# A graph layer with gathered rows: one more engine stops loading rows, and the gathers run further ahead

## The chip, the cores and the metric

The kernel runs on one core of a Trainium2 chip. A core has five engines that work side by side and wait for each other through semaphores: TensorE (PE in the profile; PEld is its weight load), VectorE (DVE), ScalarE (ACT), GpSimd (POOL) and SyncE (SP, which here only issues DMAs). The metric is the device time of one execution in microseconds; the median of three is given.

## The reference: what is computed

There are 12,500 nodes with 128 features each (x), and 200,000 directed edges (src, dst), sorted by dst. Per layer:

```
h    = max(layernorm(x), 0)                       # 12500 x 128
agg  = segment_sum(h[src], dst)                   # sum of the rows of all incoming edges
agg  = agg / max(deg, 1)                          # mean; deg counts the incoming edges
h    = relu(agg @ Wg + h @ Ws + bg)               # 128 -> 128
h    = tanh(h @ W1 + b1)                          # 128 -> 512
h    = tanh(h @ W2 + b2)                          # 512 -> 512
out  = x + h @ W3 + b3                            # 512 -> 128
```

The costly part is h[src]: 200,000 rows of 512 bytes, fetched in an order that only the data knows.

## The kernel before

**Table.** The layer norm is computed for all nodes in pieces and written to a table in DRAM, htab. All fetches of h[src] read it, so no row can be fetched from it before its last piece is written.

**Chunks.** The edges are cut into 1,563 chunks (NCH) of 128. For each chunk, the 128 rows h[src] come to lie on the 128 partitions of a tile, and a one-hot matrix (built by DVE from dst, eight chunks, a group, at a time) says which node each row belongs to. One PE matmul (line 297, function `add`) then adds the rows to the sums of a window of nodes, in PSUM. Because the edges are sorted, chunk c's window lies near node 8c; a window that touches two blocks goes to an `edge` sum first, which `merge` adds to both later. In the trace each such fp32 matmul shows as two passes.

**How rows arrive.** There are four ways.

- 80 chunks (10 groups of eight, in steps of 40 chunks from chunk 256) are `raw`: POOL gathers rows of x itself, while the table isn't ready yet, and DVE and ACT normalize them afterwards (`centre`, `factors`, `raw_scaled`).
- Most chunks are gathered from the table by POOL, one indirect DMA of 128 rows for each (function `gather`, line 310). The tiles come from a pool of AHEAD buffers, and a gather is recorded when `behind`, the count of such chunks added, is less than AHEAD back.
- 23 chunks (`slow_s`) are loaded by SP, one plain DMA for each row (function `row_loads`): the row's address is read into a register (line 344) and the row is copied (line 306).
- 15 chunks (`slow_a`) are loaded in the same way by ACT (line 335).

The lists of slow chunks are laid out at the head of `windowed`. The calls of `next(loading, 0)` and `next(loading_a, 0)` in the main loop spread the row loads: SP's come 32 at a time, ACT's four at a time. Each kind has two buffers.

**Blocks and layers.** The nodes are cut into blocks of 512 (at the end smaller ones). When all chunks of a block are added, its layers (`part0` to `part4`) are woven into PE's order, two or so matmuls between chunk matmuls. `count` sums the one-hots into degrees and takes their reciprocal; `own` loads a block's own rows from the table on SP and `own_turned` transposes them on PE (line 300), since h @ Ws needs them with features on partitions. The own rows of the next block are loaded 52 chunks, and turned 10 chunks, before the end of a span of 64 chunks, with one buffer (`hb`).

**What sets the order.** PE's matmuls, ACT's operations and SP's DMAs (`pe`, `act`, `sp_dma`) are kept in the order in which the loop records them. POOL's queue holds the 80 raw gathers and then all the others. From chunk QUICK = 1376 on, the loop weaves by a small model of time, in which the k-th gather arrives at 7.5 + 1.251 k us. A store of a block's output is recorded LATE = 12 chunks after its result. A block's layers are recorded LEAD = 10 chunks after its last chunk, if that lies before QUICK.

Of the kernel before, what the change touches and what calls it, by code (L numbers as in the profile page):

```python
# [22 lines left out]
F32 = mybir.dt.float32  # L23
# [8 lines left out]
P = 128  # L32
EPS = 1e-5
CPR = 16
BLK = 512
PIECE = 14
GRP = 8
NRAW = 10
RAW0 = 256
STEP = 40  # L40
AHEAD = 32
SLOW0 = 120
EACH = 58
EACH_A = 76
TOGETHER = 4
LOADS = 32
LATE = 12
LEAD = 10
QUICK = 1376

WINDOWS = ((0, 144), (1496, 88), (1536, 56), (1552, 40))
# [9 lines left out]
def windowed(ctx, tc, x, src, dst, Wg, Ws, bg, W1, b1, W2, b2, W3, b3, out, flag):  # L61
    nc = tc.nc
    N, D = x.shape
# [18 lines left out]
    def raw(c):  # L82
        return RAW0 <= c < RAW1 and (c - RAW0) % STEP < GRP


    slow_s, slow_a = [], []
    ns, na = 0, EACH // 2
    for c in range(SLOW0, NCH - 12):
        if raw(c):
            continue  # L90
        if ns <= 0:
            slow_s.append(c)
            ns = EACH
        elif na <= 0 and c < QUICK:
            slow_a.append(c)
            na = EACH_A
        else:
            ns -= 1
            na -= 1
    slow = slow_s + slow_a  # L100


    def first(w, span=per):
# [8 lines left out]
    blocks, n = [], 0  # L112
# [7 lines left out]
    dram = ctx.enter_context(tc.tile_pool(name="dram", bufs=1, space=bass.MemoryType.DRAM))  # L120
    const = ctx.enter_context(tc.tile_pool(name="const", bufs=1))
    raws = ctx.enter_context(tc.tile_pool(name="raws", bufs=1))
    rows_one = ctx.enter_context(tc.tile_pool(name="rows_one", bufs=2))
    rows_in = ctx.enter_context(tc.tile_pool(name="rows_in", bufs=AHEAD))
    ps_c = ctx.enter_context(tc.tile_pool(name="ps_c", bufs=1, space=PSUM))
    ps_a = ctx.enter_context(tc.tile_pool(name="ps_a", bufs=2, space=PSUM))
# [7 lines left out]
    for t, a in ((rsrc, src), (rdst, dst)):  # L134
        a = a[RAW0 * P : RAW1 * P].rearrange("(u e) -> u e", u=NRAW)[:, : GRP * P]
# [13 lines left out]
    raw_rows = []  # L149
# [29 lines left out]
    def spread(f, k):  # L179
        return f[:, :, None].to_broadcast([P, k, D])  # L180

    def centre(pool, xt, k, stats):
        nc.vector.tensor_reduce(stats[:, 0], xt, AX.X, ALU.add)
        nc.vector.scalar_tensor_tensor(xt, spread(stats[:, 0], k), -1.0 / D, xt, op0=ALU.mult, op1=ALU.add)
        sq = pool.tile([P, k, D], F32, name=f"sq{k}")
        nc.scalar.activation(sq, xt, AF.Square)
        nc.vector.tensor_reduce(stats[:, 1], sq, AX.X, ALU.add)

# [7 lines left out]
    with tc.tile_pool(name="setup", bufs=1) as sp, tc.tile_pool(name="ln", bufs=2) as ln:  # L196
# [32 lines left out]
        for i, (t0, k) in enumerate(pieces):  # L229
            xt = ln.tile([P, PIECE, D], F32, name="xt", bufs=3)  # L230
# [9 lines left out]
            stats = ps_a.tile([P, BLK], F32, name="agg")[:, : 2 * k].rearrange("p (s t) -> p s t", s=2)  # L240
            xt = xt[:, :k]
# [14 lines left out]
        for c0, w in WINDOWS[1:]:  # L256
            v = low[:, c0:]
# [31 lines left out]
    ed = ctx.enter_context(tc.tile_pool(name="ed", bufs=3))  # L289
    ml = ctx.enter_context(tc.tile_pool(name="ml", bufs=2))  # L290
# [14 lines left out]
    def sp_dma(*a):  # L305
        tc.keep_in_program_order(nc.sync.dma_start(*a))  # L306
# [10 lines left out]
    ROWB = 4 * D  # L317
    hbytes = htab.rearrange("n d -> (n d)").bitcast(U8)
# [3 lines left out]
    place = const.tile([len(slow), P], I32, name="place")  # L322
    nc.vector.tensor_scalar(place, at_i, float(ROWB), None, op0=ALU.mult)

    class act:
# [5 lines left out]
        def copy(*a):  # L331
            tc.keep_in_program_order(nc.scalar.copy(*a))  # L332

        def dma(*a):
            tc.keep_in_program_order(nc.scalar.dma_start(*a))  # L335

    def row_loads(chunks, engine, dma, name, together):
        for c in chunks:
            i = slow.index(c)
            r = rows_one.tile([P, D], F32, name=name)  # L340
            rows_t[c] = r
            rb = r.bitcast(U8)
            for p0 in range(0, P, LOADS):
                loads, vs = nc.values_load_multi_w_load_instructions(  # L344
                    place[i : i + 1, p0 : p0 + LOADS], engines=[engine], min_val=0, max_val=(N - 1) * ROWB,
                    skip_runtime_bounds_check_because="src holds rows of x, as the indirect DMAs take it to",
                )
                for ld in loads:
                    tc.keep_in_program_order(ld)
                for p, v in enumerate(vs, p0):  # L350
                    dma(rb[p : p + 1, :], hbytes[bass.ds(v, ROWB)].rearrange("(o b) -> o b", o=1))
                    if (p + 1) % together == 0:
                        yield

    def raw_stats(i):
        return stats_raw[:, :, i * GRP : (i + 1) * GRP]

    def raw_scaled(i):
        h = raw_rows[i]
        scale(h, h, GRP, raw_stats(i))  # L360
        for j in range(GRP):
            rows_t[RAW0 + i * STEP + j] = h[:, j]
# [32 lines left out]
    reach = [[] for _ in blocks]  # L395
# [84 lines left out]
    def own(s):  # L480

        n0 = s * BLK
        n = min(BLK, N - n0)
        k = -(-n // P)
        hb = ml.tile([P, BLK // P, D], F32, name="hb", bufs=1)
        sp_dma(hb[:, :k], htab[n0 : n0 + k * P, :].rearrange("(t p) d -> p t d", p=P))
        owns[s] = hb

    def own_turned(s):

        k = -(-min(BLK, N - s * BLK) // P)
        hb = owns.pop(s)
        pt = ps_t.tile([P, BLK // P, P], F32, name="pt")
        for t in range(k):
            pe.transpose(pt[:, t, :], hb[:, t, :], ident)
        hT = ml.tile([P, BLK], F32, name="hT")
        act.copy(hT[:, : k * P], pt[:, :k, :].rearrange("p t n -> p (t n)"))
        hTs[s] = hT
# [96 lines left out]
    def one_by_one(*parts):  # L595
        for part in parts:
            yield from part()

    def layers(b, before):
# [3 lines left out]
        last = [] if before is None else [part(part3, before), part(part4, before)]  # L603
        if reach[b][-1] + LEAD < QUICK:
            return one_by_one(
# [4 lines left out]
        )  # L610

    order = [c for c in range(NCH) if not raw(c) and c not in slow]
    loading = row_loads(slow_s, mybir.EngineType.SP, sp_dma, "srows", LOADS)
    loading_a = row_loads(slow_a, mybir.EngineType.Activation, act.dma, "arows", TOGETHER)
    work, done, nxt, behind = [], 0, 0, 0
    ngrp = -(-NCH // GRP)
    span = BLK // per
    now = at = 0

    def store(upto):  # L620
        while stores and stores[0][0] <= upto:
            sp_dma(*stores.pop(0)[1:])
# [5 lines left out]
    def go_on(w):  # L628
        nonlocal now
        if w:  # L630
# [3 lines left out]
            if w[1] is None:  # L634
                work.remove(w)

    own(0)
    own_turned(0)
    onehot(0)
    onehot(1)  # L640
    counted = 0
    for c in range(NCH):
        g = c // GRP
        at = c
        store(c if c >= QUICK else c - LATE)
        if c % GRP == 0 and g + 2 < ngrp:
            onehot(g + 2)
            if raw((g + 2) * GRP):
                raw_scaled(((g + 2) * GRP - RAW0) // STEP)
            if 2 <= g < 2 + NRAW:  # L650
                centre(ed, raw_rows[g - 2], GRP, raw_stats(g - 2))
            if g == 2 + NRAW:
                factors(stats_raw)

        while c % GRP == GRP // 2 and counted < len(blocks) and reach[counted][-1] // GRP <= g + 1:
            count(counted)
            counted += 1
        while nxt < len(order) and nxt < behind + AHEAD:
            gather(order[nxt])
            nxt += 1  # L660
        if not raw(c) and c not in slow:
            behind += 1
            batch = behind * P // (EACH * LOADS)
            if behind > SLOW0 - 2 * EACH and batch > (behind - 1) * P // (EACH * LOADS):
                next(loading, 0)
            batch = behind * P // (EACH_A * TOGETHER)
            if behind > 48 and batch > (behind - 1) * P // (EACH_A * TOGETHER):
                next(loading_a, 0)
        if c >= QUICK:

            there = 7.5 + 1.251 * (NRAW * GRP + order.index(c)) if c not in slow else 0
            while soonest() and max(now, soonest()[2]) < there:
                go_on(soonest())
            now = max(now, there) + 0.27
        add(c)

        lead = LEAD if c < QUICK else 2
        if done < len(blocks) and (c - lead if across[done] else c) >= reach[done][-1]:
            if across[done]:
                merge(done)  # L680
            quick = reach[done][-1] + LEAD >= QUICK

            before = done - 1 if done and reach[done - 1][-1] + LEAD < QUICK else None
            work.append([layers(done, before), 0, 0, 0, quick and blocks[done][1] <= P])
            done += 1
        if (c // span + 1) * BLK < N:
            if c % span == span - 52:
                own(c // span + 1)
            if c % span == span - 10:
                own_turned(c // span + 1)  # L690
        if c < QUICK:
            if c % 2 == 0:
                go_on(work[0] if work else None)
        if c == QUICK:
            for b, (_, n) in enumerate(blocks):
                if n < BLK:
                    own_part(b)
# [379 lines left out]
```

## Time and profile before

| what | value |
|---|---|
| median of three executions | 1931.07 us (1930.7 to 1931.43) |
| profiled execution, device time | 1931.2 us |
| its span, first to last instruction | 1928.7 us |
| PE / DVE / ACT / POOL busy | 67% / 55% / 12% / 75% |
| gathers from the table on POOL | 1,445 |
| row loads on SP / on ACT | 2,944 / 1,920 |
| mean granted PE clock | 0.866 |
| DMA, mean rate | 72 GB/s |

How to read the profile: "idle before" of a group is the time for which its engine stood idle just before those instructions, with what was released last; a line number is that of the kernel before, and one line can be that of a helper which records many operations, so tiles tell more than lines. `rows` are gathered tiles, `srows` and `arows` those loaded by SP and ACT, `hb` own rows, `raw` the rows of x. For an indirect DMA, POOL's busy time is the time it takes to issue it; the data land later. The digits of a slice are tenths of busy time in one fortieth of the span.

### The profile page before, as it was taken

How to read it: one execution, taken by the hardware profiler on the slowest of the kernel's cores; microseconds unless marked ns; L12 is line 12 of the kernel's file. 1: busy time of each engine (PE TensorE's matmuls, PEld its weight loads, DVE VectorE, ACT ScalarE, POOL GpSimd, SP SyncE). 2: the span in 40 equal slices, each digit the busy share in tenths (PEclk: the TensorE clock that was granted, in tenths of full speed). 3: DMA queues.
4: the chain of work that ended last, by engine and by line, in shares of the span. 5: the costliest groups of instructions: out<-in, count | busy, mean ns of one | idle time of the engine just before them, and what ended most of it. 6: DMA issues, size and time to landing. Idle time of an engine off the chain costs nothing.

```text
span 1928.7 us, 24991 instructions
## 1 busy us (share of the span) xinstructions
PE 1299.0 (67%) x5212; PEld 819.1 (42%) x5212; DVE 1066.8 (55%) x651; ACT 228.1 (12%) x362; POOL 1442.0 (75%) x1533
## 2 busy tenths in 40 slices
PE   0056487775757678758775676566776746878787
PEld 0034354443535445534443344344443424554466
DVE  7964865555556856636544465354554536645430
ACT  1100111010101111111100110001101101101122
POOL 7777777777777777777777777777777777777774
PEclk9999688898878888888887898878988879879698
DMA  8822222222222222222222222222222222222221
GB/s 202 233 65 53 55 67 59 61 71 60 67 71 66 66 70 67 71 71 61 65 61 66 71 61 65 61 71 66 61 66 66 61 70 61 71 78 71 66 62 40
DMA packets 128692, 139.69 MB, mean 72 GB/s; under 512 B 35036, under 2 KB 103294, under 8 KB 128336
## 3 DMA queue, kind: packets, MB, share of 16 engines
q0 software_dynamic: 48800, 100.04, 20.5%
q1 hardware_dynamic: 72654, 33.65, 6.4%
q10 hardware_dynamic: 7076, 4.32, 0.9%
q14 instruction: 119, 0.97, 0.2%
q8 instruction: 43, 0.70, 0.2%
HBM read 125.07 MB, written 12.82 MB: 71 GB/s over the span
## 4 chain that ended last, share of the span: by engine, by line
DMA 31%; PE 28%; issue 17%; SPq 11%; DVE 5%; POOL 3%; ACTq 3%; ACT 1%; POOLq 0%; DVEq 0%
PE pm L297 16%; DMA rows<-htab,scol 16%; SPq L306 10%; PE agg L297 6%; DMA arows<-htab 5%; PE edge L297 4%; DMA srows<-htab 4%; POOL rows L310 3%; DMA hb<-htab 3%; ACTq L335 3%; DVE cnt L392 2%; DMA xt<-in_x_dram 2%; PE pt L300 1%; DVE oh L382 1%; SPq L344 1%
## 5 line engine op out<-in xcount | busy, mean ns | idle before, releaser
L310 POOL DMA_INDIRECT rows<-htab,scol x1445 | 1363.4, 944 | 440.8 <-issue 258.9
L297 PE MATMUL pm<-h,w 128*128 128x512 f32 (+4 forms) x1344 | 649.1, 580 | 26.3 <-ACT h L329 26.3
L297 PE MATMUL agg<-oh,rows 128*128 128x144 f32 (+3 forms) x2068 | 484.4, 342 | 219.9 <-DMA rows<-htab,scol 217.1
L297 PEld LDWEIGHTS agg<-oh,rows 128*128 128x128 f32 x2068 | 360.7, 215 | 530.1 <-DMA rows<-htab,scol 395.2
L382 DVE TENSOR_TENSOR oh<-shared,dloc 128x1152 f32<-128x1152 f32 (+2 forms) x186 | 243.4, 1314 | 605.8 <-PE edge L297 354.9
L392 DVE TENSOR_REDUCE cnt<-oh 128x200 bf16<-128x1600 f32 (+2 forms) x186 | 525.8, 2832 | 5.4
L297 PEld LDWEIGHTS pm<-h,w 128*128 128x128 f32 x1344 | 223.4, 206 | 42.2 <-ACT h L329 29.4
L297 PEld LDWEIGHTS edge<-oh,rows 128*128 128x128 f32 x822 | 150.3, 219 | 160.5 <-issue 85.8
L297 PE MATMUL edge<-oh,rows 128*128 128x144 f32 (+2 forms) x822 | 181.8, 333 | 39.7 <-DMA rows<-htab,scol 39.4
L300 PE MATMUL pt<-ident,hb 128*128 128x128 f32 x98 | 24.5, 398 | 242.7 <-DMA hb<-htab 242.7
L329 ACT ACTIVATE h<-pm,b2c 128x512 f32<-128x512 f32 (+4 forms) x112 | 70.8, 632 | 447.6 <-PE pm L297 229.3
L300 PEld LDWEIGHTS pt<-ident,hb 128*128 128x128 f32 x98 | 16.8, 204 | 246.3 <-issue 246.3
L153 POOL DMA_INDIRECT raw<-in_x_dram,rsrc x80 | 77.7, 971 | 25.4 <-issue 23.8
L329 ACT ACTIVATE h<-pm,b1c 128x512 f32<-128x512 f32 (+4 forms) x112 | 69.9, 632 | 203.2 <-PE pm L297 107.3
L419 DVE RECIPROCAL rd<-rd 128x512 f32<-128x512 f32 (+4 forms) x28 | 81.8, 2920 | 0.0
L332 ACT COPY hT<-pt 128x512 f32<-128x512 f32 (+1 forms) x25 | 14.4, 577 | 410.2 <-PE pt L300 383.9
L589 DVE TENSOR_TENSOR o<-pt,xb 128x512 f32<-128x512 f32 x23 | 15.8, 688 | 75.9 <-PE pt L300 75.9
L417 DVE TENSOR_SCALAR rd<-pm 128x512 f32<-128x512 f32 (+4 forms) x28 | 17.2, 616 | 63.1 <-PE pm L297 63.1
L212 PE MATMUL pm<-ident,idx_f 98*128 98x98 f32 x32 | 6.2, 376 | 62.0 <-DVE idx_f L208 55.7
L297 PE MATMUL pm<-mT,wg 128*128 128x512 f32 (+4 forms) x56 | 32.6, 669 | 22.7 <-DVE mT L533 22.5
L329 ACT ACTIVATE h<-pm,bgc 128x512 f32<-128x512 f32 (+4 forms) x28 | 17.7, 632 | 240.0 <-PE pm L297 144.1
L297 PE MATMUL pm<-hT,ws 128*128 128x512 f32 (+4 forms) x56 | 34.8, 711 | 0.0
(72 smaller groups left out, 496.9 us busy)
## 6 DMA issues: line engine op xcount, KB each, us to landing
srows<-htab SPq DMA_DIRECT2D x2944, 0.5 KB
arows<-htab ACTq DMA_DIRECT2D x1920, 0.5 KB
rows<-htab,scol POOLq DMA_INDIRECT x1445
hb<-htab SPq DMA_DIRECT2D x24, 256.0 KB
xb<-in_x_dram SPq DMA_DIRECT2D x23, 256.0 KB
out_dram<-o SPq DMA_DIRECT2D x23, 256.0 KB
htab<-h SPq DMA_DIRECT2D x6, 896.0 KB
xt<-in_x_dram SPq DMA_DIRECT2D x5, 896.0 KB
```

The lines of the kernel that those rows point to most:

```text
L153: nc.gpsimd.indirect_dma_start(out=t[:, j, :], out_offset=None, in_=x, in_offset=bass.IndirectOffsetOnAxis(ap=rsrc[:, g, j : j + 1], axis=0),)
L297: tc.keep_in_program_order(nc.tensor.matmul(*a, **k))
L300: tc.keep_in_program_order(nc.tensor.transpose(*a, **k))
L306: tc.keep_in_program_order(nc.sync.dma_start(*a))
L310: nc.gpsimd.indirect_dma_start(out=r, out_offset=None, in_=htab, in_offset=bass.IndirectOffsetOnAxis(ap=scol[:, c : c + 1], axis=0),)
L329: tc.keep_in_program_order(nc.scalar.activation(*a, **k))
L335: tc.keep_in_program_order(nc.scalar.dma_start(*a))
L344: loads, vs = nc.values_load_multi_w_load_instructions(place[i : i + 1, p0 : p0 + LOADS], engines=[engine], min_val=0, max_val=(N - 1) * ROWB,
L382: nc.vector.tensor_tensor(oh[:, :k, :w], lane[:, None, :w].to_broadcast([P, k, w]), dloc[:, g * GRP : g * GRP + k][:, :, None].to_broadcas ...
L392: nc.vector.tensor_reduce(cnt[:, :n], shifted, AX.X, ALU.add)
L417: nc.vector.tensor_scalar(rd[:, :m], dg[:, :m], 1.0, None, op0=ALU.max)
L419: nc.vector.reciprocal(rd[:, :m], rd[:, :m])
```

## The change

- ACT loads no rows. SP loads 18 chunks instead of 23: from chunk 160 on, one chunk in 73 that isn't raw. All others that were slow are gathered by POOL.
- SP's row loads are recorded four at a time, spread over EACH = 72 gathered chunks for each slow chunk, beginning three times EACH ahead by the loop's condition. The tiles have four buffers.
- AHEAD goes from 32 to 48.
- LEAD goes from 10 to 16: a block's edge sums are merged, and its layers begun, six chunks later.
- Before QUICK, a block's degrees are counted one group later.
- The own rows of a block are loaded a whole span of 64 chunks before they are turned, with two buffers; two loads are issued at the start.
- The squares of the raw groups (`sq8`) have one buffer instead of two.

```diff
-AHEAD = 32
-SLOW0 = 120
-EACH = 58
-EACH_A = 76
+AHEAD = 48
+SLOW0 = 160
+EACH = 72
-LEAD = 10
+LEAD = 16
...
-    slow_s, slow_a = [], []
-    ns, na = 0, EACH // 2
+    slow, n = [], 0
     for c in range(SLOW0, NCH - 12):
         if raw(c):
             continue
-        if ns <= 0:
-            slow_s.append(c)
-            ns = EACH
-        elif na <= 0 and c < QUICK:
-            slow_a.append(c)
-            na = EACH_A
+        if n <= 0:
+            slow.append(c)
+            n = EACH
         else:
-            ns -= 1
-            na -= 1
-    slow = slow_s + slow_a
+            n -= 1
...
-    rows_one = ctx.enter_context(tc.tile_pool(name="rows_one", bufs=2))
+    rows_one = ctx.enter_context(tc.tile_pool(name="rows_one", bufs=4))
...
-    def centre(pool, xt, k, stats):
+    def centre(pool, xt, k, stats, bufs=2):
...
-        sq = pool.tile([P, k, D], F32, name=f"sq{k}")
+        sq = pool.tile([P, k, D], F32, name=f"sq{k}", bufs=bufs)
...
-    def row_loads(chunks, engine, dma, name, together):
-        for c in chunks:
-            i = slow.index(c)
-            r = rows_one.tile([P, D], F32, name=name)
+    def row_loads():
+        for i, c in enumerate(slow):
+            r = rows_one.tile([P, D], F32, name="srows")
...
-                    dma(rb[p : p + 1, :], hbytes[bass.ds(v, ROWB)].rearrange("(o b) -> o b", o=1))
-                    if (p + 1) % together == 0:
+                    sp_dma(rb[p : p + 1, :], hbytes[bass.ds(v, ROWB)].rearrange("(o b) -> o b", o=1))
+                    if (p + 1) % TOGETHER == 0:
                         yield
...
-        hb = ml.tile([P, BLK // P, D], F32, name="hb", bufs=1)
+        hb = ml.tile([P, BLK // P, D], F32, name="hb", bufs=2)
...
     own(0)
+    own(1)
     own_turned(0)
...
-                centre(ed, raw_rows[g - 2], GRP, raw_stats(g - 2))
+                centre(ed, raw_rows[g - 2], GRP, raw_stats(g - 2), bufs=1)
...
-        while c % GRP == GRP // 2 and counted < len(blocks) and reach[counted][-1] // GRP <= g + 1:
+        while c % GRP == GRP // 2 and counted < len(blocks) and reach[counted][-1] // GRP <= g + (c >= QUICK):
             count(counted)
...
-            batch = behind * P // (EACH * LOADS)
-            if behind > SLOW0 - 2 * EACH and batch > (behind - 1) * P // (EACH * LOADS):
+            batch = behind * P // (EACH * TOGETHER)
+            if behind > SLOW0 - 3 * EACH and batch > (behind - 1) * P // (EACH * TOGETHER):
                 next(loading, 0)
-            batch = behind * P // (EACH_A * TOGETHER)
-            if behind > 48 and batch > (behind - 1) * P // (EACH_A * TOGETHER):
-                next(loading_a, 0)
...
-        if (c // span + 1) * BLK < N:
-            if c % span == span - 52:
-                own(c // span + 1)
-            if c % span == span - 10:
-                own_turned(c // span + 1)
+        if c % span == span - 10 and (c // span + 1) * BLK < N:
+            own_turned(c // span + 1)
+            if (c // span + 2) * BLK < N:
+                own(c // span + 2)
```

More of the change, by code (lines that the diff above doesn't have):

```diff
@@ L332, in copy @@
             tc.keep_in_program_order(nc.scalar.copy(*a))
-        def dma(*a):
-            tc.keep_in_program_order(nc.scalar.dma_start(*a))
-    def row_loads(chunks, engine, dma, name, together):
-        for c in chunks:
-            i = slow.index(c)
-            r = rows_one.tile([P, D], F32, name=name)
+    def row_loads():
+        for i, c in enumerate(slow):
+            r = rows_one.tile([P, D], F32, name="srows")
             rows_t[c] = r
@@ L344, in row_loads @@
                 loads, vs = nc.values_load_multi_w_load_instructions(
-                    place[i : i + 1, p0 : p0 + LOADS], engines=[engine], min_val=0, max_val=(N - 1) * ROWB,
+                    place[i : i + 1, p0 : p0 + LOADS], engines=[mybir.EngineType.SP], min_val=0,
+                    max_val=(N - 1) * ROWB,
                     skip_runtime_bounds_check_because="src holds rows of x, as the indirect DMAs take it to",
@@ L612, in windowed @@
     order = [c for c in range(NCH) if not raw(c) and c not in slow]
-    loading = row_loads(slow_s, mybir.EngineType.SP, sp_dma, "srows", LOADS)
-    loading_a = row_loads(slow_a, mybir.EngineType.Activation, act.dma, "arows", TOGETHER)
+    loading = row_loads()
     work, done, nxt, behind = [], 0, 0, 0
```

## The prediction

> **What bounds the kernel now.** I read the page's busy times first, then the costliest groups, then what GpSimd (POOL) waited for, then single stretches of POOL's timeline, and only then the other engines' waits.
>
> ```profile
> span 1928.7 us, 24991 instructions
> PE 1299.0 (67%) x5212; PEld 819.1 (42%) x5212; DVE 1066.8 (55%) x651; ACT 228.1 (12%) x362; POOL 1442.0 (75%) x1533
> ...
> POOL 7777777777777777777777777777777777777774
> ...
> L310 POOL DMA_INDIRECT rows<-htab,scol x1445 | 1363.4, 944 | 440.8 <-issue 258.9
> ```
>
> POOL is the busiest engine, but 75% looks like an engine with a quarter to spare. It has none. The digits are flat at 7 in 39 of 40 slices, and the gathers' row has 440.8 us of idle time over 1,445 gathers, 0.305 us each. What POOL waited for tells whether that is a fixed cost or slack:
>
> ```profile
> POOL rows L310 <- issue: 258.9, 849, 0.3
> POOL rows L310 <- PE agg L297: 79.0, 259, 0.3
> POOL rows L310 <- PE edge L297: 36.3, 119, 0.3
> POOL rows L310 <- PE pm L297: 34.8, 114, 0.3
> POOL rows L310 <- DMA rows<-htab,scol: 26.0, 85, 0.3
> ```
>
> The columns are total, times and longest. Whatever is named as releaser, no wait is longer than 0.3 us: the names are only what happened to finish last inside the same fixed gap. One gather therefore costs 0.944 + 0.305 = 1.249 us and the next begins at once. The timeline shows the same where the gathers of raw x end and those of the table begin:
>
> ```profile
> 102.46 0.94 POOL L153 DMA_INDIRECT raw<-in_x_dram,rsrc  x1 [0.30 <-issue]
> 103.71 0.94 POOL L153 DMA_INDIRECT raw<-in_x_dram,rsrc  x1 [0.30 <-issue]
> 104.96 0.94 POOL L310 DMA_INDIRECT rows<-htab,scol  x1 [0.30 <-DVE cnt L392]
> ```
>
> There is no gap for the layer norm: its last table write is over at 91.24 us (86.73 + 4.51 in the chain of waits), 13.7 us before POOL comes to need it. So POOL works without a break from its first gather at 2.9 us to its last at 1908.0 us. The first table gather starts at 104.96 and the last at 1907.99, 1,444 periods apart: 1.24864 us each. Two stretches, 1200 to 1500 us and 1789 us to the end, check that nothing stretches it:
>
> ```profile
> L310 POOL DMA_INDIRECT rows<-htab,scol x241: 940/944/953, 1200.1 to 1499.7; - x121
> ```
>
> ```profile
> L310 POOL DMA_INDIRECT rows<-htab,scol x97: 940/944/953, 1788.2 to 1908.0; - x97
> ```
>
> In the first, both SyncE (SP) and ScalarE (ACT) issue row loads; 299.6 us over 240 periods is 1.2483 us. In the second neither does (their last starts are 1788.8 and 1605.7); 119.8 over 96 is 1.2479.
>
> The kernel's time is thus a count: 105 us of start, 1,445 gathers at 1.24864 us, and 20.7 us from the start of the last gather to the end of the span (landing, the last block's layers, the store, the flag). The chain of waits hides this, and the reader should see why:
>
> ```profile
> DMA 31%; PE 28%; issue 17%; SPq 11%; DVE 5%; POOL 3%; ACTq 3%; ACT 1%; POOLq 0%; DVEq 0%
> ```
>
> It follows the last event before each step, so at every 0.3 us gap it jumps to whatever had just finished. Engines that merely keep step with POOL collect the shares.
>
> **The change, part by part.**
>
> *Chunks that leave SP and ACT.* Before, 23 chunks are loaded by SP (2,944 rows / 128) and 15 by ACT (1,920 / 128). The new loop, one chunk in 73 that isn't raw from chunk 160 on, gives 18: 160, 233, 322, 411, 508, 597, 678 and every 73rd from there to 1481. There are 1,563 chunks and 80 are raw, so gathers go from 1,563 - 80 - 38 = 1,445 to 1,563 - 80 - 18 = 1,465. Twenty more gathers, all on POOL's unbroken queue: 20 x 1.24864 = +24.97 us. This is the one term on the path.
>
> A rule of the Trainium skill would price this otherwise. "DMA: Bandwidth & Descriptors", section "Issuing engines are not separate DMA queues", says that DMAs from all issuing engines share the same 16 DMA engines, and that issuing from several at once saves only the issuing time, usually small beside the transfer. If transfers were the limit, dropping ACT as an issuer would cost about nothing and the sum would be 1931. The trace speaks against using it so here: issuing is the limit itself.
>
> *Work taken off SP and ACT.* ACT loses 1,920 loads and SP 640, with their index reads. ACT was computing 12% of the time; SP's remaining 2,304 loads at the observed pace (32 in 10.69 us at 671.20, 0.334 us each) are 770 us of a span of over 1,900. Both lie beside POOL: 0. At the start ACT issues 20 fewer index-row loads, which can only bring the table forward, and POOL does not reach it before 104.96 anyway: 0. The second early load of own rows (256 KB) is issued after the table writes: 0.
>
> *Own rows a span earlier, two buffers.* This goes at the largest waits that look mendable:
>
> ```profile
> PE pt L300 <- DMA hb<-htab: 242.7, 19, 31.4
> ...
> SPq L306 <- DMA arows<-htab: 397.1, 270, 40.0
> ```
>
> The first is TensorE (PE) waiting in its queue for the own-row tile, 242.7 us in all; the second is SP held up among row loads, the own-row load behind them. At 685.04 us PE takes up its transposes after 19.14 us of such idleness, and SP had issued that tile's load only at 682.00, behind 32 row loads. With the load a whole span earlier, these PE waits should nearly vanish. What is late next is what PE already waits for most: freshly gathered rows (395.2 us at the weight loads), that is, POOL. So up to 240 us of PE waiting turns into waiting for POOL, and the time gains 0. PE's 31 us stalls never reached POOL because the row buffers covered them. I paired the 1,445 gathers with the 2,890 row matmuls (two passes per chunk) in order: a buffer came free at the least 2.8 us before POOL took it again, at 693 us, just behind that stall; mostly 15 to 36 us before.
>
> *48 row buffers instead of 32.* They add 16 x 1.249 = 20 us of cover to a queue that never waited: 0 gained. They also make a new stall less likely: PE must fall 48 x 1.249 = 60 us behind, where before no row matmul starts more than 36 us after its gather's end.
>
> *Row loads with four buffers, four rows at a time.* A chunk's loads are spread over 72 steps and done 88 gathered chunks (110 us) before its matmul; a buffer is asked for 128 chunks after its last use. SP does not wait, and the stores or own loads standing between get through after four rows rather than 32: 0. If this cover failed, PE would stand still and POOL after 60 us.
>
> *Merging at 16 instead of 10 chunks, counts a group later, one square buffer.* These move PE and VectorE (DVE) work later within slack: DVE is 55% busy, PE 67%. The single buffer makes the next square wait for the reduction of the last; ten raw groups at 1.22 us bound it at 12 us, on engines with idle time: 0, while PE stays under 60 us of lag.
>
> *The tail.* From the last 20 chunks on PE's order is that of before, and the planner's arrival time for a chunk grows by 20 x 1.251 = 25.02 us, as the gathers' does. No trace shows how PE's clock will stand there: before, PE is busy 6.58 of 7 us at a granted 0.76 just after 1908 us, then 6.53 of 8 us at 1.00. All 13.1 us at 1.00 would gain 1.6 us; all at 0.76 would lose 2.1 us. I take 0, since the order is the same.
>
> **Sum.** 104.96 + 1,464 x 1.24864 = 1932.97 us for the start of the last gather, + 20.7 = 1953.7 us of span, + 2.5 around it (1931.2 - 1928.7) = 1956.2 us. The profiled 1931.2 lies 0.13 above the median of 1931.07, so: 1956.0 us, 1.3% slower.
>
> **Rivals.**
>
> *Not slower: POOL's period shrinks.* If the 2,560 loads that go away were what stretches a gather, or if the 0.305 us gap were a wait on some busy resource, each gather would be faster. For 1931 us it must fall by 25 / 1,465 = 17 ns, to 1.2316 us. For it: POOL and the loads share DMA engines, busy about 25%. Against: with no row loads at all the trace has 1.2479 us, worth 0.0007 x 1,465 = 1.1 us, so 1955. I give it 2%, shared with anything between.
>
> *The removed PE waits pay.* The chain puts 2.9% of the span, 56 us, on own rows. Were PE the bound, that would give 1956 - 56 = 1900 us. It decides only if POOL had been held by full buffers, and its longest gap is 0.3 us: 1%.
>
> *A new stall reaches POOL.* If PE's largest lag (36 us) and its longest wait (31.4) fell together, 67 us would pass the 60 us of cover and hold POOL for about 7.5 us: 1963.5. A row chunk or a store that blocks SP could do it. The 110 us of lead speaks against it: 5%.
>
> *The tail goes otherwise.* PE's clock (-1.6 to +2.1 us, above), or up to 1 us of matmuls queued when the last rows land, moves the end: 1954.4 to 1959, inside the range.
>
> **How the numbers follow.** The forecast with its tail has 92%, the three others 2, 1 and 5. Low end: 1956.0 less the tail's 1.6 and the period's 1.1, 1953.3. High end: the tail's +3.1 and 1.4 of a stall's 7.5, 1960.5. Less than 0.2% of the time (3.9 us), about what a measurement tells from no change, would need a gain of 21 us from what I cost at 0: faster 2%, same 1%, slower 97%.
>
> **What would show it.** Right: 1,465 gathers with a period of 1.2486 us and no POOL wait above 0.3 us, the last starting near 1933.0; own-row waits of PE near 0, its waits for gathered rows up by as much; the tail 20 to 21 us. Wrong: a POOL wait of microseconds (a stall), a period off by over 1 ns, or the first table gather not at 105 us.

## The result, and the profile after

| | before | after |
|---|---|---|
| median | 1930.88 us (1930.55 to 1931.43, 4 executions) | 1955.1 us (1954.24 to 1955.8, 4 executions) |
| profiled execution | 1931.2 us | 1955.45 us |
| its span | 1928.7 us | 1953.5 us |
| gathers from the table | 1,445 | 1,465 |
| mean granted PE clock | 0.866 | 0.913 |

The change makes the kernel slower by 24.2 us: ratio 1.0125, 95% interval 1.0107 to 1.0142. In four of the six sets of experiment runs the kernel before itself took 2615 to 2640 us on the chip that was used; where that is so it is said, and each kernel is compared with the kernel before on the same chip in the same set.

The page of the changed kernel, its span, busy times, POOL's slices, the gathers' group and the engines of the chain:

```profile
span 1953.5 us, 19720 instructions
...
PE 1382.7 (71%) x5212; PEld 821.2 (42%) x5212; DVE 1069.3 (55%) x651; ACT 229.9 (12%) x362; POOL 1461.5 (75%) x1553
...
POOL 7777777777777777777777777777777777777774
...
issue 34%; DMA 28%; PE 25%; POOL 11%; DVE 2%; ACT 0%; POOLq 0%; ACTq 0%
...
L303 POOL DMA_INDIRECT rows<-htab,scol x1465 | 1383.6, 944 | 446.6 <-issue 291.4
```

The gathers now stand at line 303. Their idle time is 446.6 us over 1,465, 0.305 us each as before, and POOL's slices are as flat. The chain's shares changed a good deal (SP had 11% before and is gone), while what bounds the kernel didn't.

What POOL waited for in the changed kernel (total, times, longest), and its timeline where the table's gathers begin:

```profile
POOL rows L303 <- issue: 291.4, 956, 0.3
POOL rows L303 <- PE agg L290: 61.9, 203, 0.3
POOL rows L303 <- DMA rows<-htab,scol: 39.1, 128, 0.3
```

```profile
103.24 0.94 POOL L146 DMA_INDIRECT raw<-in_x_dram,rsrc  x1 [0.30 <-issue]
104.49 0.94 POOL L303 DMA_INDIRECT rows<-htab,scol  x1 [0.30 <-issue]
```

No wait of these gathers is longer than 0.3 us. The last gather starts at 1933.40, so the period is (1933.40 - 104.49) / 1,464 = 1.24925 us.

PE's waits for gathered rows (the first column is the total) and for own rows, and then SP's largest wait, after:

```profile
PEld agg L290 <- DMA rows<-htab,scol: 583.5, 748, 2.2
PE agg L290 <- DMA rows<-htab,scol: 312.6, 473, 2.0
PE edge L290 <- DMA rows<-htab,scol: 112.5, 170, 2.8
...
PE pt L293 <- DMA hb<-htab: 32.5, 1, 32.5
```

```profile
SPq L299 <- DVE o L579: 799.4, 25, 74.4
```

The same waits of PE's chunk matmuls for gathered rows, before:

```profile
PE agg L297 <- DMA rows<-htab,scol: 217.1, 338, 6.8
...
PE edge L297 <- DMA rows<-htab,scol: 39.4, 69, 1.6
```

PE's waiting for own rows fell from 242.7 us to 32.5 us, one wait before the first block. Its chunk matmuls wait for gathered rows instead: 312.6 + 112.5 = 425.1 us, where before it was 217.1 + 39.4 = 256.5. That is 169 us more of waiting for POOL for 210 us less of waiting for own rows. SP's 397.1 us of waiting that names ACT's row loads are gone; it waits 799.4 us for results to store.

### The profile page after: what moved, and what is told of

Its sections match the earlier page's. It is cut to its first block, busy times and chain, and to the rows that moved or that the text cites. A ratio compares the mean times of both kernels' runs of the same rounds, so it can differ in the third digit from the quotient of the medians.

```text
span 1953.5 us, 19720 instructions
## 1 busy us (share of the span) xinstructions
PE 1382.7 (71%) x5212; PEld 821.2 (42%) x5212; DVE 1069.3 (55%) x651; ACT 229.9 (12%) x362; POOL 1461.5 (75%) x1553
## 4 chain that ended last, share of the span: by engine, by line
issue 34%; DMA 28%; PE 25%; POOL 11%; DVE 2%; ACT 0%; POOLq 0%; ACTq 0%
DMA rows<-htab,scol 28%; PE pm L290 14%; PE agg L290 8%; POOL rows L303 8%; POOL raw L146 4%; PE edge L290 3%; PE pt L293 1%; DVE cnt L382 1%; DVE oh L372 0%; ACT h L322 0%; DVE rd L409 0%; DMA raw<-in_x_dram,rsrc 0%; ACT sq L179 0%; DMA rsrc<-in_src_dram 0%; DVE o L579 0%
## 5 line engine op out<-in xcount | busy, mean ns | idle before, releaser
L303 POOL DMA_INDIRECT rows<-htab,scol x1465 | 1383.6, 944 | 446.6 <-issue 291.4
L290 PE MATMUL agg<-oh,rows 128*128 128x144 f32 (+3 forms) x2098 | 554.1, 363 | 327.9 <-DMA rows<-htab,scol 312.6
L290 PEld LDWEIGHTS agg<-oh,rows 128*128 128x128 f32 x2098 | 378.5, 222 | 692.8 <-DMA rows<-htab,scol 583.5
L290 PE MATMUL pm<-h,w 128*128 128x512 f32 (+4 forms) x1344 | 633.9, 569 | 13.8 <-ACT h L322 13.7
L290 PE MATMUL edge<-oh,rows 128*128 128x144 f32 (+2 forms) x832 | 206.3, 343 | 113.0 <-DMA rows<-htab,scol 112.5
L290 PEld LDWEIGHTS edge<-oh,rows 128*128 128x128 f32 x832 | 143.7, 209 | 268.8 <-DMA rows<-htab,scol 227.9
L293 PE MATMUL pt<-ident,hb 128*128 128x128 f32 x98 | 19.8, 338 | 39.5 <-DMA hb<-htab 32.5
L290 PE MATMUL pm<-hT,ws 128*128 128x512 f32 (+4 forms) x56 | 43.3, 871 | 0.0
L322 ACT ACTIVATE h<-pm,b3c 128x512 f32<-128x512 f32 (+4 forms) x28 | 17.7, 633 | 178.4 <-PE pm L290 178.4
L523 DVE TENSOR_TENSOR mT<-agg,rd 128x512 f32<-128x512 f32 (+4 forms) x28 | 17.3, 618 | 29.0 <-PE agg L290 28.7
```

What stands on the lines that cost most here:

```text
L290: tc.keep_in_program_order(nc.tensor.matmul(*a, **k))
L293: tc.keep_in_program_order(nc.tensor.transpose(*a, **k))
L303: nc.gpsimd.indirect_dma_start(out=r, out_offset=None, in_=htab, in_offset=bass.IndirectOffsetOnAxis(ap=scol[:, c : c + 1], axis=0),)
L322: tc.keep_in_program_order(nc.scalar.activation(*a, **k))
L523: nc.vector.tensor_tensor(mT[:, :n], acc[b][:, :n], rds.pop(b)[:, :n], op=ALU.mult)
```

## The experiments

Theory G: the time is the count of gathers at 1.249 us each, on a POOL queue that never waits. Rival W: the loss comes from the other parts of the change. A third view was that the PE waits which went away are worth time.

**The chunk lists alone.** The kernel before with the change's 18 chunks on SP and none on ACT; buffers, leads, own rows, batches of 32 and the merge stay as before.

```diff
-SLOW0 = 120
-EACH = 58
-EACH_A = 76
+SLOW0 = 160
+EACH = 72
+EACH_A = 10**6
...
-    ns, na = 0, EACH // 2
+    ns, na = 0, EACH_A
```

> The kernel before with one edit: the list of slow chunks is that of the change (18 on SP, none on ACT), so 1,465 chunks are gathered; buffers, leads, own rows and batches of 32 stay as before. Theory G (the time is the count of gathers at 1.249 us each on a queue that never waits): 1931 + 20 x 1.249 = 1956 us, POOL's longest wait 0.3 us, PE's waits for own rows still over 100 us. Rival W (the loss comes from the rest of the change: later merging, SP held up behind stores for 799 us): 1931 us.

Measured: 2312.5 us, but the kernel before took 2639.6 us on that chip (ratio 0.8748, 0.8696 to 0.8799). Neither theory had that; it is taken up below. The same kernel was measured on another chip.

> The kernel of the first experiment again (the kernel before with the change's 18 slow chunks on SP and nothing else), because in the first call the kernel before itself took 2640 us on that chip, not 1931, and SP, ACT and PE took up instructions in steps of about 0.7 us. Where the kernel before takes 1931 us: theory G says 1956 us with no POOL wait over 0.3 us; rival W says 1931 us. Where it takes about 2640 us again: 2312 us again.

Measured: 1955.64 us where the kernel before took 1929.94 (ratio 1.0132, 1.0103 to 1.0162). Profile of this kernel: its span, its gathers, PE's waits for own rows and SP's two largest waits:

```profile
span 1953.0 us, 19745 instructions
...
L310 POOL DMA_INDIRECT rows<-htab,scol x1465 | 1382.9, 944 | 446.6 <-issue 276.2
```

```profile
PE pt L300 <- DMA hb<-htab: 31.7, 1, 31.7
```

```profile
SPq L306 <- PE agg L297: 353.6, 11, 38.8
SPq L306 <- DVE o L589: 332.8, 18, 61.4
```

The lists alone give the whole loss: 25.7 us against 24.2 us for the whole change. G holds and W falls: what the rest of the change is worth is lost in the spread of the runs (the kernel before alone spans 3.3 us here). The two profiles agree closely: the last gather starts at 1932.96 us with the lists alone and at 1933.40 us with the whole change, and both spans end 20.1 us later. With 32 buffers the longest wait of a table gather is 0.3 us here too.

One part of the expectation was wrong: that PE's waits for own rows would stay over 100 us. They went to 31.7 us, though own rows are loaded as late as before and into one buffer. The trace points to ACT's row loads as what held them up before: with them, SP's largest wait was for the DMAs of `arows` (397.1 us); without them no such wait is listed. How one queue can wait for the other can be followed in the trace of the kernel before. The DMAs of SP and ACT signal their landing on the same eight semaphores, and every SP wait that names `arows` is for one of these. The longest, 40.0 us, ends at 169.12 us: SP's next row load uses a semaphore that an ACT row load, issued at 167.78 us, had raised at 169.10 us, and ACT's first row load was issued only at 166.2 us. That ACT's loads and not the number of SP's matter rests on these rows; the edit also takes five chunks from SP, and no run separates the two.

**The rest alone.** The changed kernel with the lists and ACT loads of before (23 chunks by SP, 15 by ACT).

```diff
-SLOW0 = 160
-EACH = 72
+SLOW0 = 120
+EACH = 58
+EACH_A = 76
...
+        def dma(*a):
+            tc.keep_in_program_order(nc.scalar.dma_start(*a))
...
+            batch = behind * P // (EACH_A * TOGETHER)
+            if behind > 48 and batch > (behind - 1) * P // (EACH_A * TOGETHER):
+                next(loading_a, 0)
```

> The changed kernel with the chunk lists of before: 23 chunks by SP (four rows at a time) and 15 by ACT, so 1,445 gathers; 48 buffers, LEAD 16, later counts and early own rows as in the change. Theory G: 1955.1 - 20 x 1.249 = 1930 us, although PE's waits for own rows are nearly gone (before: 242.7 us). Rival W: stays at 1955 us. A third view, that the removed PE waits pay once the extra gathers are out of the way: well under 1931, by up to 56 us.

> The kernel of the second experiment again (the changed kernel with the 23 + 15 row-loaded chunks of before, so 1,445 gathers), where the kernel before takes 1931 us. Theory G: 1930 us, although PE's waits for own rows fall from 242.7 us to near 33. Rival W: 1955 us. The removed PE waits pay: well under 1931.

> The kernel of the second experiment a last time (the changed kernel with the 23 + 15 row-loaded chunks of before, so 1,445 gathers). Where the kernel before takes 1931 us: theory G says 1930 us. Since the experiment with the chunk list alone has shown PE's waits for own rows to go when ACT's row loads go, they should be back here, at 150 us or more, in spite of two buffers and a load one span ahead; if early loading were what removed them, they would stay near 33 us. Where the kernel before takes about 2630 us: about the same as the kernel before.

Measured, all three on chips where the kernel before took 2615 to 2640 us: 2643.71, 2627.44 and 2621.71 us, ratios 1.0006 (0.9976 to 1.0036), 1.0012 (0.9972 to 1.0053) and 1.0015 (0.9988 to 1.0042). So on those chips the rest makes no measurable difference. Where the kernel before takes 1931 us this kernel has not been measured; that the rest is worth nothing there is concluded from the chunk lists alone and the whole change, which take the same time within the spread. The third measurement's waits for own rows:

```profile
PE pt L300 <- DMA hb<-htab: 380.1, 16, 31.7
```

Two buffers and a load one span ahead do not remove these waits while ACT loads rows, as the last expectation had it. This is seen on a chip of the 2615 us kind; at 1931 us the kernel with more row loads, below, shows the same (283.7 us).

**Fewer buffers.** The kernel before with AHEAD = 24 instead of 32, and the changed kernel with 24 instead of 48. The edit of the first:

```diff
-AHEAD = 32
+AHEAD = 24
```

> The kernel before with 24 row buffers instead of 32, nothing else. The pairing of gathers and matmuls gives a least slack of 2.8 us at 693 us and 7.2 us near 576 us; eight buffers fewer take 10 us from each. Theory G with its cover: POOL is held 7 us near 693 us and about 3 us near 576 us, and the time is 1931 + 7 to 12 = 1938 to 1943 us, with POOL waits of microseconds. Rival (PE's waits for own rows never get near POOL): 1931 us.

> The kernel of the third experiment again (the kernel before with 24 row buffers instead of 32), where the kernel before takes 1931 us. Theory G with its cover: POOL is held about 7 us near 693 us and about 3 us near 576 us; 1938 to 1943 us, with POOL waits of microseconds. Rival (PE's waits for own rows never get near POOL): 1931 us.

> The changed kernel with 24 row buffers instead of 48, nothing else. In its trace a buffer comes free at the least 36.4 us before it is taken again; 24 buffers fewer take 30 us of that. Theory G: 6 us are left, no POOL wait over 0.3 us, 1955 us. Rival (the deeper gathers are needed): POOL waits of microseconds and over 1958 us.

> The kernel of the fourth experiment again (the changed kernel with 24 row buffers instead of 48), where the kernel before takes 1931 us. Theory G: least slack 36.4 - 30 = 6 us, no POOL wait over 0.3 us, 1955 us. Rival (the deeper gathers are needed): POOL waits of microseconds and over 1958 us.

All four ran on chips where the kernel before took 2640 or 2620 us. The kernel before with 24 buffers: 2637.52 and 2617.33 us, ratios 0.9992 (0.9965 to 1.0019) and 0.9994 (0.995 to 1.0038). The changed kernel with 24: 2327.09 and 2314.57 us, ratios 0.8805 (0.8745 to 0.8865) and 0.881 (0.8741 to 0.888). The question that they were made for, whether 24 buffers hold POOL up at 1931 us, stays open. They do show that the changed kernel, with 24 buffers, takes about 0.88 of the time of the kernel before on those chips, like the chunk lists alone at 0.875.

**More row loads instead of fewer.** The changed kernel with 27 chunks on SP and 19 on ACT, so 1,437 gathers; the rest as in the change.

```diff
-SLOW0 = 160
-EACH = 72
+SLOW0 = 120
+EACH = 50
+EACH_A = 60
```

> The changed kernel with more row loads on both queues instead of fewer: 27 chunks on SP (one in 51) and 19 on ACT (one in 61, four buffers), so 1,437 gathers; all else as in the change. Theory G: 1955.1 - 28 x 1.249 = 1920 us, if both queues keep up (a chunk's 128 row loads took at best 52 us on SP, and the spacing is 62 us). Rival (PE, ACT or the queues are then the limit): 1930 us or more, with POOL waits of microseconds.

Measured: 2732.03 us where the kernel before took 2620.36 (ratio 1.0406, 1.0344 to 1.0468). The same kernel was measured on another chip.

> The kernel of the experiment with more row loads again (the changed kernel with 27 chunks loaded by SP and 19 by ACT, 1,437 gathers). Where the kernel before takes 1931 us: theory G says 1955.1 - 28 x 1.249 = 1920 us with no POOL wait over 0.3 us; the rival (PE, ACT or the queues are then the limit) 1930 us or more, with POOL waits of microseconds. Where the kernel before takes about 2630 us: 2732 us again, about 14 us for each row-loaded chunk more.

Measured: 1950.46 us (1945.79 and 1955.14) where the kernel before took 1929.5 (ratio 1.011, 1.0049 to 1.0172). The gathers of this kernel in the profile (first and last start, us), two waits, and the busy times by stretch (PE, PEld, DVE, ACT, POOL, then PE's clock, DMA share and GB/s):

```profile
L310 POOL DMA_INDIRECT rows<-htab,scol x1437: 940/944/961, 104.6 to 1897.9; - x180
```

```profile
PE pt L300 <- DMA hb<-htab: 283.7, 18, 25.1
...
SPq L306 <- DMA arows<-htab: 231.4, 237, 41.0
```

```profile
1790.00:1898.00 108.00, 61.03 (x304) 45.03 (x304) 42.12 (x43) 13.41 (x25) 81.48 (x88) 0.78 0.27 70
1898.00:1943.00 45.00, 36.15 (x288) 33.96 (x286) 6.27 (x20) 14.19 (x42) 0.84 (x1) 0.94 0.05 14
```

This is the instructive miss. POOL did what G says: its last gather starts at 1897.9 us, 35.5 us sooner than in the changed kernel, for 28 gathers fewer (28 x 1.249 = 35.0), and no wait of a table gather is above 0.3 us. But PE was behind by then. When each gather is paired with its matmuls, PE's median lag is 8 us in the first third of the gathers, 24 us in the second and 40 us in the last, and at most 57 us. At the tightest point a buffer came free 1.2 us before its next gather took it. After the last gather PE still works for 40 us, and the span's end comes 45.6 us after that gather's start, not 20.1. So of the 35.5 us won on POOL, 25.5 us were lost again in the tail. This holds for the profiled execution of 1945.79 us; the other took 9 us more, and its tail isn't known.

What made PE late is not isolated by a run, but the rows point to it: PE waits 283.7 us for own rows, and SP waits 231.4 us for ACT's row loads. The longest stop can be followed, on PE and then on SP:

```profile
1788.71 2.13 PE L297 MATMUL agg<-oh,rows 128*128 128x144 f32 x16
1832.84 1.09 PE L300 MATMUL pt<-ident,hb 128*128 128x128 f32 x4 [42.00 <-DVE o L590]
```

```profile
1783.21 19.49 SPq L306 DMA_DIRECT2D srows<-htab  x52
1802.80 0.41 SPq L306 DMA_DIRECT2D hb<-htab  x1
1805.53 23.34 SPq L306 DMA_DIRECT2D srows<-htab  x64
1828.92 0.41 SPq L306 DMA_DIRECT2D xb<-in_x_dram  x1
```

At 1790.84 us PE finishes a run of chunk matmuls and then stands 42 us, to 1832.84, before it turns the next own rows. The PSUM tile for it is held by the previous block's result, which needs rows of x (`xb`) that SP issued only at 1828.92, after 52 and 64 row loads. So G has a limit: the count gives the time only while PE isn't behind at the last gather.

**Three chunks more than before.** As the last, with 24 on SP (none after chunk 1480) and 17 on ACT.

```diff
-EACH = 50
-EACH_A = 60
+EACH = 52
+EACH_A = 68
...
-        if ns <= 0:
+        if ns <= 0 and c < 1480:
```

> The changed kernel with 24 chunks on SP (one in 53, none after chunk 1480) and 17 on ACT (one in 69), so 1,442 gathers: three row-loaded chunks more than before, and the last 120 chunks free of row loads so that PE can catch up. Where the kernel before takes 1931 us: theory G with a tail of 20 us says 1955.1 - 23 x 1.249 = 1926 us. Rival (ACT's row loads hold SP up, own rows and rows of x come late, and PE is behind when the last gather is issued, as with 46 chunks): 1931 us or more, with a tail over 25 us. Where the kernel before takes about 2630 us: about 2680 us.

Measured: 2650.24 us where the kernel before took 2619.64 (ratio 1.0159, 1.0092 to 1.0227), less than the 2680 us expected for such chips. What it does at 1931 us is open. No kernel of this study beat the kernel before where that takes 1931 us.

**The chips on which the kernel before takes 2615 to 2640 us.** SP's row-loading instructions (ns, min/median/max), in the kernel with the chunk lists alone on such a chip (2312.5 us), and then in the kernel before at 1931 us:

```profile
L306 SPq MOVE srows<-htab x2304: 2/29/1408, 108.3 to 2094.5; - x192
L306 SPq DMA_DIRECT2D srows<-htab x2304: 2/224/1397, 109.7 to 2095.2; - x192
```

```profile
L306 SPq MOVE srows<-htab x2944: 29/29/29, 103.4 to 1788.7; - x197
L306 SPq DMA_DIRECT2D srows<-htab x2944: 224/228/387, 103.5 to 1788.8; - x197
```

The median move takes 29 ns in both, but on the first chip a move takes up to 1,408 ns. The median from the start of one row load to the next is 0.709 us instead of 0.324, and 21% of the steps from one SP instruction's start to the next lie between 0.64 and 0.76 us, against 0.4%. It isn't the kernel that differs: with the chunk lists alone at 1955.64 us every move takes 29 ns too, and the median step is 0.323 us. That kernel's mean granted PE clock is 0.79 on the first chip against 0.90 there; whether that is a cause or a consequence isn't shown. The gather itself is unchanged (a median of 945 ns), but POOL is no longer unbroken:

```profile
POOL rows L310 <- issue: 322.6, 1018, 4.3
POOL rows L310 <- remote: 195.1, 131, 4.7
POOL rows L310 <- PE agg L297: 141.1, 150, 9.8
```

There the trade has the other sign: 20 row-loaded chunks fewer take 327 us away (2639.6 - 2312.5), 16 us a chunk; 8 more cost 112 us (2732.0 - 2620.4), 14 us a chunk; and 3 more cost 31 us (2650.2 - 2619.6), 10 us a chunk. Row loads aren't all of it: after SP's last row load, at 2095.2 us, gathers still come only every 1.43 us on average. Why instructions are taken up so slowly there was not found out.

## Why the prediction was right

**The bound.** "The kernel's time is thus a count" holds, with each term near: first gather 104.49 us (foretold 104.96), 1,465 gathers at 1.24925 us (1.24864), last start 1933.40 (1932.97), tail 20.1 us (20.7), around the span 1.95 us (2.5). The sum is 1955.45 us for the profiled execution instead of 1956.2. The difference is about -0.5 us of start, +0.9 of period, -0.6 of tail and -0.5 around the span; each is smaller than the spread of the four executions (1.6 us). The period of the chunk lists alone was 1.24879, so the 0.6 ns are no property of the change that these runs show.

**Twenty more gathers, +24.97 us.** Shown in isolation: 25.7 us with the chunk lists alone. On POOL the issuing time, 1.249 us a gather, is the kernel's time. The Trainium skill's rule ("DMA: Bandwidth & Descriptors", section "Issuing engines are not separate DMA queues") is that issuing from several engines at once saves only the time to initiate the DMA, usually small beside the DMA itself. Read with that "usually", ACT's exit would have been priced at about nothing; the measured 25.7 us shows that this case is not the usual one.

**Own rows: 0, waits nearly gone.** The number and the worth were right. The reason was wrong in the step "With the load a whole span earlier, these PE waits should nearly vanish". They vanish with the chunk lists alone (31.7 us, old loading), and where ACT still loads rows they stay, in spite of the new loading (380.1 us in the rest alone, on a chip of the 2615 us kind; 283.7 us with more row loads). That they vanished as forecast was luck: another part of the same change did it.

**48 buffers: 0.** Right. The least time between a buffer's last use and its next gather went from 2.8 to 36.4 us. Not all of that is the 16 buffers' 20 us: with 32 buffers and the chunk lists alone it is 19.4 us, where PE's lag is at most 19 us instead of 36.

**"SP does not wait".** Wrong as stated. SP waited 799.4 us, 25 times, up to 74.4 us, for blocks' results that it has to store, and the row loads behind each store waited with it. It cost nothing: the last load of each chunk was still issued 111 to 195 us before the chunk's matmul (110 us were foretold), and PE's weight loads waited for `srows` 0.4 us in all.

**The tail.** PE's granted clock was 0.73 in the 7 us from 1933 us, then 1.00 in the next 8, against 0.76 and 1.00 before. The bounds of -1.6 and +2.1 us were not needed.

**The rivals.** POOL's period didn't shrink when 2,560 row loads went; the removed PE waits didn't pay; no stall reached POOL. The stall's near miss is the kernel with more row loads, where PE's lag of up to 57 us left 1.2 us of the cover, and PE's lateness was paid at the end instead. That the kernel may run where POOL is not the bound at all was in no case of the prediction.

## What to carry to other kernels

An engine that shows 75% busy can be full: divide its idle time by its instructions, look at the longest wait, and check that the period is the same in stretches with different company. Work moved onto such an engine is priced by its period, and waits removed elsewhere were worth nothing here, since that engine never waited for them; work moved off it pays only while the others are not late when its last instruction is issued. And when a wait disappears together with the edit that aims at it, make the other edits alone before giving that edit the credit.

## What the runs showed of the hardware that I had not expected

- SP's queue waited for ACT's row loads: 397.1 us of SP's waits before name the DMAs of `arows`, none after ACT stopped, and the DMAs of both queues signal on the same eight semaphores. That ACT's row loads are late because they stand behind activations that wait for PE is argued from the order of its instructions, not shown.
- The kernel before takes 1931 us on some chips and 2615 to 2640 us on others, and a change that loses 1.3% on the first kind wins 12.5% on the second (the chunk lists alone, 0.8748), where SP's moves take up to 1,408 ns instead of 29. Of the five chips whose numbers were recorded none was seen in both kinds, at one or two times each, so whether this belongs to the chip or to the time of the run is open.
